# First group of a two-layer graph kernel: another order of loads, copies and sums; the last group's bias added in DRAM by one transfer

## The chip, the cores and the metric

The kernel runs on one core of one Trainium2 chip. The metric is the device time of one execution in microseconds (us); lower is better. The core has five engines that run side by side, each through its own list of instructions in order: PE (TensorE, matrix products; its loading of weights is listed apart as PEld), DVE (VectorE), ACT (ScalarE), POOL (GpSimd) and SP (SyncE, which here only issues transfers). ACT and POOL issue transfers too, between their other instructions. PE has a granted clock, which the profile gives as a share of full speed.

## The reference, cut to what matters

```python
# layer 0, four heads of 128; x is 4096 x 512, adj 4096 x 4096 of zeros and ones
support = (x @ weight) split in heads
f1, f2  = support . weight_u, support . weight_v          # one number per row and head
w       = leaky_relu(f1[column] + f2[row], 0.2) * adj
attn    = softmax(where(w != 0, w, -1e30)) * (w != 0)
x1      = layernorm(x + attn @ support + bias + x @ proj_w + proj_b)
# layer 1, eight heads of 64: masked attention on x1 with Wks, Wqs, Wvs, Wo
out     = layernorm(x1 + attention(x1, max(adj, eye)))
```

The change touches only the part before and at the start of layer 0's attention: `support`, the two dot products, and `base = x + x @ proj_w + bias + proj_b`, which is kept in DRAM and added when a window of rows is closed.

## The kernel before, in words

**Groups.** The 4096 rows are worked in eight groups `g` of 512 (loop L910). A group makes two products: kind "s" (`x @ weight`, into a tile `s4`) and kind "b" (`x @ (proj_w + I)`, into two tiles `base[0]` and `base[1]`; the identity, added to `proj_w` once by `add_identity`, stands for the `x +`). Each product is done by seven block products instead of eight (Strassen's scheme in Winograd's form), numbered 1 to 7. Products 1, 2, 4 (of x) and 1, 2, 3 (of the weights) use plain blocks, the others sums of blocks: four sums of x for each group (`combine_x`, numbers 0 and 1 on DVE, 2 and 3 on POOL) and four sums of the weights for each kind (`combine_w`), made once. `product` (L835) issues the eight matrix instructions of a block product as 2 x 2 calls at L846 and then its end: products 1 and 5 are copied from PSUM to SBUF by ACT (L863), product 2 by ACT to its place (L865), 6, 7, 3, 4 are added to what went before by DVE (L867, L869, L874), and POOL adds product 5 to one block (L871). Products 2, 3 and 4 add to the PSUM tiles of 1, 5 and 7, so product 2 cannot start before ACT has copied 1, nor 4 before DVE has read 7.

**Order.** The order of every engine is the order in which the program is written (`manual_schedule`). A list `plan` gives the order of the fourteen products of a group: `begin` for the first group, `usual` for the middle ones, `end` for the last. `beside`, `todo` and `early` hang other work on places in the plan: loads of the adjacency, the dot products (`dots`, eight pairs of instructions at L817 for each of four blocks, on DVE), the transposes of the next group's x (`turn_x`, DVE), and for the last group the first work of the attention (`signs` on ACT, `front` on DVE). `later` puts a piece of work a few steps on.

**First loads.** x and the weights come in quarters of 32 partitions. ACT's queue issues the first half of `weight` (four transfers), one quarter of x, the second half of `weight` (L664), then `weight_u`, `weight_v` and `bias`, each spread to all partitions (L676, L677). SP's queue issues the rest of the first group's x, `proj_w` (eight transfers) and the next group's x. [...] PE runs 46 idle transposes (L886) until the first data are there. The weights' sums of kind "s" are on DVE (L763), those of kind "b" on POOL after the identity (sixteen instructions at L895); POOL then adds `proj_b` to `bias` by an adding transfer (L905).

**Bias.** The sum `bb` of the two biases is added to `base[0]` and `base[1]` of each group at L879: by POOL, and in the last group by DVE. Each is then stored by SP (L881).

**Hand-over to the attention.** The attention of layer 0 goes over passes (window `w` of 1024 rows, head `h`) and 32 steps `j` in each. `front(w, h, j)` makes the tile of weights `p` of a step: two steps of signs on ACT (L624), a mask on DVE (L635), and one DVE instruction for each tile (L640); four tiles exist (`LA + 1`). `front` runs three steps ahead of PE's products (L1087): the first three tiles are made in the last group (`early`), the fourth in the first round of the loop at L1076. The adjacency goes through DRAM: POOL's transfer turns it to bf16 (`narrow`, L586), SP's transposes it into `stage` (`turn_in0`, L594), ACT shrinks it to fp8 (`shrink`, L600). Of the first window's eight pieces the last (piece 7) is issued by `beside_unit` in the first round of the loop; its transpose stands in SP's list behind that of piece 6, and `shrink` of pieces 6 and 7 stands in ACT's list among the signs.

Of the kernel before, what the change touches and what calls it, by code (L numbers as in the profile page):

```python
# [8 lines left out]
F32 = mybir.dt.float32  # L9
# [3 lines left out]
AF = mybir.ActivationFunctionType  # L13
ALU = mybir.AluOpType
# [4 lines left out]
P = 128  # L19
# [410 lines left out]
def tile_gat_then_masked_attention(  # L430
# [16 lines left out]
    nc = tc.nc  # L447
    N, D = x.shape
# [4 lines left out]
    NG = N // G  # L453
    GT = G // P
# [15 lines left out]
    NQ = P // SQ  # L470
# [33 lines left out]
    def on_all_partitions(src, n):  # L504
        return bass.AP(tensor=src.tensor, offset=src.offset, ap=[[0, P], [1, n]])
# [61 lines left out]
    with tc.tile_pool(name="l0", bufs=NG) as l0, \  # L567
# [3 lines left out]
        LA = 3  # L571
# [73 lines left out]
        with tc.tile_pool(name="l0s", bufs=2) as sp:  # L645
# [11 lines left out]
                        x[g * G + b0 * SQ:g * G + b1 * SQ, a * P:(a + 1) * P].rearrange(  # L657
                            "(b r) f -> r b f", r=SQ))

            def load_w0(queue, dst, src, c):  # L660

                for a in range(NQ):
                    f = a * P + 2 * c * SQ
                    queue.dma_start(  # L664
                        dst[a * SQ:(a + 1) * SQ, 2 * c:2 * c + 2, :],
                        src[f:f + 2 * SQ, :].rearrange("(k r) d -> r k d", r=SQ))
# [1 line left out]
            bb = sp.tile([P, D], F32, name="bb", bufs=1)  # L668
            load_w0(nc.scalar, w_sb, weight, 0)
            load_x(0, 0, HG // SQ, (nc.sync, nc.sync, nc.sync, nc.scalar))  # L670
            load_w0(nc.scalar, w_sb, weight, 1)
            load_x(0, HG // SQ, G // SQ)
            for c in range(2):
                load_w0(nc.sync, pw_sb, proj_w, c)
            for k, src in enumerate((weight_u, weight_v)):
                nc.scalar.dma_start(uv[:, k, :], on_all_partitions(src, D))  # L676
            nc.scalar.dma_start(bb, on_all_partitions(bias, D))  # L677
            load_x(1)

            def factors(g, s4):  # L680
# [41 lines left out]
            for c in range(NCJ):  # L722
# [4 lines left out]
                if c < NCJ - 3:  # L727
                    for k in range(CJ):
# [1 line left out]
                            lambda c=c, k=k: shrink(0, c, k))  # L730
            beside.setdefault(NT // 2, []).append(lambda: load_fr(0, 0))
            early = {5: lambda: signs(0, 0, 0), 8: lambda: front(0, 0, 0), 9: lambda: front(0, 0, 1),
                     7: lambda: signs(0, 0, 2), 11: lambda: front(0, 0, 2)}

            def turn_x(g, c, n=0, halves=1):

# [98 lines left out]
            def product(g, s4, kind, i):  # L835

                if i in (1, 5, 6, 7):
                    tiles[kind, i] = op.tile([P, G], F32, name="o_ps")  # L840
                out = tiles[kind, {2: 1, 3: 5, 4: 7}.get(i, i)]
                more = i in (2, 3, 4)
                xb, wb = x_of(g, i), w_of(kind, i)
                for t in range(2):
                    for c in range(2):
                        nc.tensor.matmul(out[:, t * HD:(t + 1) * HD], xb[:, c, t * P:(t + 1) * P],  # L846
                                         wb[:, c, :], start=not more and t == 0 and c == 0,
                                         stop=c == 1, skip_group_check=True)
                if i == 1:
                    if kind == "b":  # L850
                        for n in range(2):
                            base[n] = sp.tile([P, 2, D], F32, name="base", bufs=3)
                    elif g == NG - 1:
                        places = room("y_sb").rearrange("p s c r -> p s (c r)")
                        sb.update({("s", 1): places[:, 0], ("s", 5): places[:, 1],
                                   ("b", 1): places[:, 2], ("b", 5): places[:, 3]})
                    else:
                        sb.update({("s", 1): room("z"), ("s", 5): room("z"),
                                   ("b", 1): room("az"), ("b", 5): room("az")})
                u2, p5 = sb[kind, 1], sb[kind, 5]  # L860
                last = block_of(kind, s4, 1, 1)
                if i in (1, 5):
                    nc.scalar.activation(sb[kind, i], out, AF.Copy)  # L863
                elif i == 2:
                    nc.scalar.activation(block_of(kind, s4, 0, 0), as_block(out, kind), AF.Copy)  # L865
                elif i == 6:
                    nc.vector.tensor_tensor(u2, out, u2, op=ALU.add)  # L867
                elif i == 7:
                    nc.vector.tensor_tensor(last, as_block(out, kind), as_block(u2, kind),  # L869
                                            op=ALU.add)  # L870
                    nc.gpsimd.tensor_tensor(last, last, as_block(p5, kind), op=ALU.add)  # L871
                else:
                    n, m = (0, 1) if i == 3 else (1, 0)
                    nc.vector.tensor_tensor(block_of(kind, s4, n, m), as_block(out, kind),  # L874
                                            as_block(u2, kind), op=ALU.add)
                if kind == "b" and i in (3, 4):
                    n = (3, 4).index(i)
                    engine = nc.vector if g == NG - 1 else nc.gpsimd
                    engine.tensor_tensor(base[n], base[n],  # L879
                                            bb[:, None, :].to_broadcast([P, 2, D]), op=ALU.add)  # L880
                    later.at(1, lambda t=base[n]: nc.sync.dma_start(  # L881
                        base_d[g][:, 2 * n:2 * n + 2, :], t))

# [3 lines left out]
            for n in range(2):  # L887
                for c in range(KC):
                    turn_x(0, c, n, 2)
            def add_identity(m):  # L890
                for c in range(KC):
                    for a in range(2 * m, 2 * m + 2):
                        q, f = slice(a * SQ, (a + 1) * SQ), a * P + c * SQ
                        d = pw_sb[q, c, f:f + SQ]
                        nc.gpsimd.tensor_tensor(d, d, ident[q, q], op=ALU.add)  # L895

            combine_x(0, 0)
            combine_w(nc.vector, "s", (5,))
            for i in (1, 2, 3):
                combine_x(0, i)  # L900
            combine_w(nc.vector, "s", (6, 7, 4))
            for m in range(2):
                add_identity(m)
# [1 line left out]
            nc.gpsimd.dma_start(bb, on_all_partitions(proj_b, D), accum_op=ALU.add)  # L905
            uv_ps = [xp.tile([P, H0, D0], F32, name="x_ps") for _ in range(2)]
            usual = [(kind, i) for i in (1, 5, 2, 6, 7, 3, 4) for kind in ("s", "b")]
            begin = [(kind, i) for kind in ("s", "b") for i in (1, 2, 5, 6, 7, 3, 4)]
            end = [(kind, i) for kind in ("s", "b") for i in (1, 5, 2, 6, 7, 3, 4)]
            for g in range(NG):  # L910
                fs[g] = l0.tile([P, 2, GT, H0], F32, name="f")
                s4 = sp.tile([P, H0, GT, W0], F32, name="s4")
                plan = end if g == NG - 1 else usual if g else begin
                todo = {}
                for k, (i, wait, n, m) in enumerate(
                        ((2, 1, 0, 0), (3, 0, 0, 1), (7, 3, 1, 1), (4, 0, 1, 0))):
                    todo.setdefault(plan.index(("s", i)) + wait if g else 7 + k, []).append((n, m))
                for k, (kind, i) in enumerate(plan):
                    if k in (0, 3, 7, 10):
                        t = (0, 3, 7, 10).index(k)  # L920
                        if t == 1 and g + 2 < NG:
                            load_x(g + 2)
                        for fn in beside.get(g * GT + t, []):
                            fn()
                    product(g, s4, kind, i)
                    if g == 0 and k == 6:
                        for n in range(2):
                            nc.scalar.activation(uv_ps[n], uv[:, n, :].rearrange(
                                "p (h d) -> p h d", h=H0), AF.Copy)
                    for nm in todo.get(k, ()):  # L930
                        dots(g, s4, *nm)
                    if g == NG - 1 and k in early:
                        early[k]()
                    if g == NG - 1 and k == 10:
                        factors(g, s4)
                    first = 0 if g else 10
                    if g + 1 < NG and first <= k < first + KC:
                        turn_x(g + 1, k - first)
                    if g + 1 < NG and (6 <= k < 10 if g else k == 13):
                        for n in (k - 6,) if g else range(4):  # L940
                            combine_x(g + 1, n)
                    if k in (2, 6, 9, 12):
                        later.step()
                xTs.pop(g)
                x_s.pop(g)
                if g + 1 == NG:
                    later.step()
                if g + 1 < NG:
                    later.at(1, lambda g=g, s4=s4: factors(g, s4))

# [33 lines left out]
        with wait_by_tile("l0v", 2) as vp:  # L984
# [91 lines left out]
            for n, (w, h, j) in enumerate(steps):  # L1076
                if n + LA < len(steps):
                    beside_unit(*steps[n + LA])
                    front(*steps[n + LA])
                if j == 0:  # L1080
                    o_t[w, h] = [op.tile([P, G], F32, name="o_ps")[:, 0:BK * W0].rearrange(
                        "p (b d) -> p b d", b=BK) for _ in range((WT + BK - 1) // BK)]
# [709 lines left out]
```

## Time and profile before

| | us |
|---|---|
| three timed runs | 3325.18, 3324.55, 3321.34 |
| their median | 3324.55 |
| the profiled execution, its own time | 3324.41 |
| span of its instructions | 3322.5 |
| PE busy in the span | 3301.6 (99%) |
| DVE, POOL, ACT busy | 2477.7, 2173.3, 1947.7 |
| group 0: first product to the start of group 1 | 8.78 to 40.96 |
| groups 1 to 7 | 40.96 to 210.17 |
| layer 0's attention | from 210.17 |

The time is the span and 1.9 us around it. A row of the timeline has start, duration, engine, line, operation, what it writes and reads, and in brackets how long the engine was idle before it and what ended that. SPq, ACTq and POOLq are issues of transfers, whose durations are those of the issue and not of the transfer. A merged row stands for several instructions (x8). In a row of the view by windows each engine has its busy time in that stretch, then come the granted clock and the share of the DMA engines.

### The profile page before, as it was taken

The numbers are of one execution on the slowest core, as the hardware profiler recorded it, in microseconds if no ns is written. First come the engines' busy times: TensorE is split into PE (matmuls) and PEld (weight loads), VectorE is DVE, ScalarE is ACT, GpSimd is POOL, SyncE is SP. The second block draws the span as 40 slices with busy tenths as digits, with TensorE's granted clock in tenths as the row PEclk, the third lists the DMA queues.
The fourth block names the chain that finished last, engine by engine and source line by source line (L and its number), as shares of the span: only waits on it lengthen the run. The fifth ranks groups of instructions, "written<-read, shape, count | busy, mean of one in ns | idle before, by whom it ended". The sixth has DMA issues, their size and how long they took to land.

```text
span 3322.5 us, 67217 instructions
## 1 busy us (share of the span) xinstructions
PE 3301.6 (99%) x27160; PEld 1967.0 (59%) x27160; DVE 2477.7 (75%) x3186; ACT 1947.7 (59%) x2439; POOL 2173.3 (65%) x1602
## 2 busy tenths in 40 slices
PE   9999999999999999999999999999999999999998
PEld 8899999999999777733333333333333333333333
DVE  6689899899999677467767666677666766667766
ACT  1267968878766310156656566566665656656564
POOL 5630040040030244389999999999999999999996
PEclk9999999999999999999999999999999999999999
DMA  8989796686532444489898988889889799897984
GB/s 178 227 204 183 220 182 170 153 191 147 138 93 58 104 146 125 153 221 208 193 211 224 228 195 198 209 188 259 198 197 211 187 215 242 196 210 185 214 195 112
DMA packets 398993, 612.06 MB, mean 184 GB/s; under 512 B 167632, under 2 KB 248528, under 8 KB 398672
## 3 DMA queue, kind: packets, MB, share of 16 engines
q0 software_dynamic: 97520, 258.77, 42.8%
q1 hardware_dynamic: 299280, 345.88, 33.5%
q8 instruction: 216, 3.54, 0.4%
q10 hardware_dynamic: 1872, 3.02, 0.4%
q14 instruction: 105, 0.86, 0.1%
HBM read 315.87 MB, written 109.25 MB: 128 GB/s over the span
## 4 chain that ended last, share of the span: by engine, by line
PE 97%; DVE 1%; DMA 1%; POOL 1%; issue 0%; ACT 0%; ACTq 0%; POOLq 0%; DVEq 0%
PE o_ps L1087 27%; PE o_ps L1599 26%; PE s_ps L1138 26%; PE o_ps L846 5%; PE s_ps L1663 3%; PE s_ps L1298 2%; PE s_ps L1248 2%; PE s_ps L1255 2%; PE x_ps L1255 1%; PE x_ps L1248 1%; PE s_ps L1618 1%; DMA p<-p 0%; PE s_ps L1294 0%; DMA w_sb<-in_L_gnn_weight_dram 0%; DVE p L1731 0%
## 5 line engine op out<-in xcount | busy, mean ns | idle before, releaser
L1574 POOL TENSOR_TENSOR q_sum<-q_sum,p 128x1024 f32<-128x1024 f32 x538 | 1375.6, 2557 | 64.3 <-DMA p<-p 39.5
L1554 DVE TENSOR_TENSOR p<-s_ps,adjT 128x1024 f32<-128x1024 f32 x896 | 1044.5, 1216 | 465.0 <-ACT s_ps L1551 436.2
L1551 ACT ACTIVATE s_ps<-s_ps 128x1024 f32<-128x1024 f32 x1021 | 967.2, 1006 | 594.4 <-PE s_ps L1138 591.9
L1599 PE MATMUL o_ps<-p,v_sb 64*64 64x512 f32 x8192 | 943.6, 590 | 0.0
L1138 PE MATMUL s_ps<-q_sb,k_sb 64*64 64x512 f32 x8192 | 942.9, 589 | 0.1
L1087 PE MATMUL o_ps<-sup_t,p 128*128 128x129 f32 x8192 | 915.7, 275 | 1.2 <-DVE p L640 1.2
L1087 PEld LDWEIGHTS o_ps<-sup_t,p 128*128 128x128 f32 x8192 | 915.3, 192 | 1.7 <-DVE p L640 1.4
L640 DVE SCALAR_TENSOR_TENSOR p<-fr_t,dj,az 128x1024 f32<-128x1024 f32 x512 | 650.3, 1284 | 66.9 <-PE o_ps L1087 38.8
L1599 PEld LDWEIGHTS o_ps<-p,v_sb 64*64 64x64 f32 x8192 | 310.3, 133 | 570.6 <-issue 560.6
L1138 PEld LDWEIGHTS s_ps<-q_sb,k_sb 64*64 64x64 f32 x8192 | 312.6, 133 | 566.4 <-issue 453.9
L624 ACT ACTIVATE z<-fr_t,f 128x1024 fp8e4<-128x1024 f32 x512 | 557.1, 1143 | 100.9 <-DVE az L635 100.8
L1584 POOL DMA_DIRECT2D p<-p x412 | 438.6, 1303 | 10.1 <-PE o_ps L1599 9.2
L1063 POOL DMA_DIRECT2D agg<-base_d x32 | 29.1, 1217 | 386.8 <-DMA sup_t<-sup_d 204.7
L585 POOL COPY seen<-token 128x1 f32<-128x1 f32 x24 | 10.9, 455 | 356.8 <-DVE token L583 356.8
L1554 DVE TENSOR_TENSOR p<-s_ps,md 128x1024 f32<-128x1024 f32 x128 | 150.7, 1217 | 67.8 <-ACT s_ps L1551 62.0
L635 DVE TENSOR_TENSOR az<-adjT,z 128x512 int32<-128x512 int32 x256 | 175.2, 685 | 2.1 <-ACT z L624 0.9
L600 ACT ACTIVATE adjT<-stage 128x1024 fp8e4<-128x1024 bf16 x128 | 130.9, 1051 | 18.3 <-DMA stage<-adj_d 18.2
L1663 PE MATMUL s_ps<-wo_sb,on 128*128 128x512 f32 x240 | 110.8, 604 | 0.0
L1633 ACT ACTIVATE r<-r_h 32x256 f32<-32x256 f32 x248 | 102.2, 412 | 2.9
L1049 ACT ACTIVATE agg<-o_ps,rinv 128x128 f32<-128x128 f32 x128 | 42.1, 370 | 70.5 <-DVE den L1042 46.3
L1322 ACT ACTIVATE v<-s_ps 128x256 f32<-128x256 f32 x28 | 10.7, 383 | 115.0 <-PE s_ps L1298 99.9
L1663 PEld LDWEIGHTS s_ps<-wo_sb,on 128*128 128x128 f32 x240 | 43.3, 189 | 55.9 <-issue 55.7
(275 smaller groups left out, 2236.0 us busy)
## 6 DMA issues: line engine op xcount, KB each, us to landing
p<-p POOLq DMA_DIRECT2D x412, 512.0 KB, 9.1
k_sb<-k_d SPq DMA_DIRECT2D x128, 512.0 KB
v_sb<-v_d SPq DMA_DIRECT2D x128, 512.0 KB
adj_d<-in_adj_dram POOLq DMA_DIRECT2D x32, 1024.0 KB, 11.0
sup_t<-sup_d SPq DMA_DIRECT2D x120, 258.0 KB
fr_t<-fr_d SPq DMA_DIRECT2D x16, 1024.0 KB
adjT_d<-adjT SPq DMA_DIRECT2D x32, 512.0 KB
adjT<-adjT_d SPq DMA_DIRECT2D x32, 512.0 KB
```

What stands on the lines that cost most here:

```text
L624: nc.scalar.activation(z[:, k, :], fr_t[w, h][:, 0, :], AF.Sign, bias=fs[j // GT][:, 0, (j + k) % GT, h:h + 1], saturate=False)
L635: nc.vector.tensor_tensor(az.bitcast(I32), adjT[w, j // CJ][:, j % CJ:j % CJ + 2, :].bitcast(I32), z.bitcast(I32), op=ALU.bitwise_and)
L640: nc.vector.scalar_tensor_tensor(p, fr[:, 1, :], dj[j // GT][:, j % GT, h:h + 1], az_t[w, h, j // 2][:, j % 2, :], op0=ALU.max, op1=ALU.mult)
L846: nc.tensor.matmul(out[:, t * HD:(t + 1) * HD], xb[:, c, t * P:(t + 1) * P], wb[:, c, :], start=not more and t == 0 and c == 0, stop=c == ...
L1087: nc.tensor.matmul(o[t // BK][:, t % BK, :], p[:, t * P:(t + 1) * P], s, start=(j == 0 and t % BK == 0), stop=(j == NT - 1), skip_group_ch ...
L1138: nc.tensor.matmul(s[c:c + MS, e, :], k[r, a + c:a + c + MS], qt[g, m][r, :], start=True, stop=True)
L1551: nc.scalar.activation(s, s, AF.Exp, scale=float(KD) ** -0.5)
L1554: nc.vector.tensor_tensor(p, s, keep[:, None, :].to_broadcast([P, HP, G]), op=ALU.mult)
L1574: nc.gpsimd.tensor_tensor(q, q, p, op=ALU.add)
L1584: later.at(2, lambda: nc.gpsimd.dma_start(a, b, accum_op=ALU.add))
L1599: nc.tensor.matmul(o[c, n, :], v[r, j % CH, c], p[r, e, :], start=(j == 0), stop=(j == NT - 1))
L1663: nc.tensor.matmul(s, on_t[g][:, m, t * P:(t + 1) * P], wo_sb[:, m, :], start=(m == 0), stop=(m == NP1 - 1))
```

## The change

- **Loads.** SP issues the first two quarters of the second half of `weight` ahead of the second half of the first x; ACT issues only the other two. `weight_u`, `weight_v` and `bias` are issued by POOL, between and after its two sums of x.
- **ACT's table.** A copy of one column (`ones`, into a small tile) is put on ACT ahead of its last two loads, so that the load of ACT's function table stands there.
- **DVE's first sum of weights** (number 5 of kind "s") stands between the transposes of the two halves of x.
- **Plan of the first group.** Kind "b" goes 1, 5, 2, 6, 7, 3, 4 instead of 1, 2, 5, 6, 7, 3, 4.
- **Last group's bias.** The two DVE additions are gone. After the group's last step POOL issues one adding transfer that adds `bb`, repeated four times, to `base_d[7]` in DRAM; it waits for the stores of both base tiles. Piece 7 of the adjacency stands behind it in POOL's list.
- **Fourth tile of weights.** `front(0, 0, 3)` is put in the last group, after product 3 of kind "b" and ahead of DVE's end of product 4; the loop's first round leaves it out.

```diff
-            def load_w0(queue, dst, src, c):
+            def load_w0(queue, dst, src, c, quarters=range(NQ)):
-                for a in range(NQ):
+                for a in quarters:
...
             load_w0(nc.scalar, w_sb, weight, 0)
             load_x(0, 0, HG // SQ, (nc.sync, nc.sync, nc.sync, nc.scalar))
-            load_w0(nc.scalar, w_sb, weight, 1)
+            load_w0(nc.sync, w_sb, weight, 1, range(2))
+            nc.scalar.activation(small.tile([P, 1], F32, name="bn_ve"), ones[:, 0:1], AF.Copy)
+            load_w0(nc.scalar, w_sb, weight, 1, range(2, NQ))
             load_x(0, HG // SQ, G // SQ)
             for c in range(2):
                 load_w0(nc.sync, pw_sb, proj_w, c)
-            for k, src in enumerate((weight_u, weight_v)):
-                nc.scalar.dma_start(uv[:, k, :], on_all_partitions(src, D))
-            nc.scalar.dma_start(bb, on_all_partitions(bias, D))
             load_x(1)
...
             early = {5: lambda: signs(0, 0, 0), 8: lambda: front(0, 0, 0), 9: lambda: front(0, 0, 1),
-                     7: lambda: signs(0, 0, 2), 11: lambda: front(0, 0, 2)}
+                     7: lambda: signs(0, 0, 2), 11: lambda: front(0, 0, 2), 12: lambda: front(0, 0, 3)}
...
                 if kind == "b" and i in (3, 4):
                     n = (3, 4).index(i)
-                    engine = nc.vector if g == NG - 1 else nc.gpsimd
-                    engine.tensor_tensor(base[n], base[n],
-                                            bb[:, None, :].to_broadcast([P, 2, D]), op=ALU.add)
+                    if g < NG - 1:
+                        nc.gpsimd.tensor_tensor(base[n], base[n],
+                                                bb[:, None, :].to_broadcast([P, 2, D]),
+                                                op=ALU.add)
...
             for n in range(2):
                 for c in range(KC):
                     turn_x(0, c, n, 2)
+                if n == 0:
+                    combine_w(nc.vector, "s", (5,))
...
             combine_x(0, 0)
-            combine_w(nc.vector, "s", (5,))
-            for i in (1, 2, 3):
+            for i in (1, 2):
                 combine_x(0, i)
+            for k, src in enumerate((weight_u, weight_v)):
+                nc.gpsimd.dma_start(uv[:, k, :], on_all_partitions(src, D))
+            combine_x(0, 3)
+            nc.gpsimd.dma_start(bb, on_all_partitions(bias, D))
             combine_w(nc.vector, "s", (6, 7, 4))
...
-            begin = [(kind, i) for kind in ("s", "b") for i in (1, 2, 5, 6, 7, 3, 4)]
             end = [(kind, i) for kind in ("s", "b") for i in (1, 5, 2, 6, 7, 3, 4)]
+            begin = [("s", i) for i in (1, 2, 5, 6, 7, 3, 4)] + end[7:]
...
                 if g + 1 == NG:
                     later.step()
+                    nc.gpsimd.dma_start(base_d[g], bb[:, None, :].to_broadcast([P, GT, D]),
+                                        accum_op=ALU.add)
...
                     beside_unit(*steps[n + LA])
-                    front(*steps[n + LA])
+                    if n:
+                        front(*steps[n + LA])
```

## The prediction

> **What bounds the kernel now.** First the page: busy times, then the chain that ended last.
>
> ```profile
> PE 3301.6 (99%) x27160; PEld 1967.0 (59%) x27160; DVE 2477.7 (75%) x3186; ACT 1947.7 (59%) x2439; POOL 2173.3 (65%) x1602
> ...
> PE 97%; DVE 1%; DMA 1%; POOL 1%; issue 0%; ACT 0%; ACTq 0%; POOLq 0%; DVEq 0%
> ```
>
> PE is the bound: it is idle 3322.5 - 3301.6 = 20.9 us in all. The first real product starts at 8.78 and the last 12 us are the closing of the kernel, neither of which the change touches. What is left is small, so I read where PE waits in the two places that the diff touches, with the timeline. The first group:
>
> ```profile
> 8.78 1.99 PE L846 MATMUL o_ps<-w_sb,xT 128*128 128x256 f32 x8
> ...
> 11.82 0.33 ACTq L677 DMA_DIRECT2D bb<-in_L_gnn_bias_dram  x1
> 12.19 1.28 ACT L863 ACT_TABLE_LOAD   x1 [12.19 <-DMA w_sb<-in_L_gnn_weight_dram]
> ...
> 13.48 0.60 ACT L863 ACTIVATE z<-o_ps 128x512 f32<-128x512 f32 x1
> 14.13 3.78 PE L846 MATMUL o_ps<-w_sb,xT 128*128 128x256 f32 x8 [3.36 <-ACT z L863]
> ```
>
> Product s1 ends at 10.77. s2 adds to the same PSUM tile and waits 3.36 us for ACT's copy, and ACT is late because its last three issues (9.52, 10.63, 11.82) each wait for a quarter of the second half of the weights, with the table load behind them. s2 then takes 3.6 us where eight instructions take 1.72 later on. The view by windows says why:
>
> ```profile
> 10.80:12.80 2.00, 0.00 (x0) 0.00 (x0) 1.20 (x4) 0.61 (x1) 0.34 (x1) 1.00 1.07 246
> 12.80:14.10 1.30, 0.00 (x0) 0.00 (x0) 1.27 (x2) 1.27 (x2) 0.92 (x1) 0.51 1.06 277
> 14.10:16.30 2.20, 2.17 (x5) 1.81 (x6) 2.20 (x5) 0.00 (x0) 0.75 (x1) 0.50 1.04 302
> 16.30:19.60 3.30, 3.30 (x9) 2.58 (x9) 2.10 (x2) 0.60 (x1) 2.94 (x7) 0.50 1.12 218
> 19.60:23.00 3.40, 3.40 (x18) 2.99 (x17) 0.60 (x1) 1.61 (x3) 2.71 (x12) 0.99 1.20 185
> ```
>
> After 2.0 us of idleness the granted clock falls to half, until 19.6; PE works from 14.13 to 19.65 at half speed and loses 5.5 / 2 = 2.7 us. What ends the group:
>
> ```profile
> 28.76 1.39 POOL L871 TENSOR_TENSOR s<-s,z 128x512 f32<-128x512 f32 x1
> ...
> 35.46 0.69 DVE L867 TENSOR_TENSOR az<-o_ps,az 128x512 f32<-128x512 f32 x1 [1.80 <-PE o_ps L846]
> 37.73 0.71 DVE L740 STREAM_TRANSPOSE xT<-y_sb 128x512 f32<-128x512 f32 x1
> 38.36 0.65 DVE L869 TENSOR_TENSOR base<-o_ps,az 128x512 f32<-128x512 f32 x1
> ...
> 39.16 1.97 PE L846 MATMUL o_ps<-more_w,xT 128*128 128x256 f32 x8 [0.35 <-DVE base L869]
> ```
>
> b4, the last product, waits for DVE. From 40.96 PE runs without a gap to the attention, whose fourth step waits:
>
> ```profile
> 214.42 1.23 DVE L879 TENSOR_TENSOR base<-base,bb 128x1024 f32<-128x1024 f32 x1 [0.56 <-POOL base L871]
> ...
> 215.56 1.28 DVE L640 SCALAR_TENSOR_TENSOR p<-fr_t,dj,az 128x1024 f32<-128x1024 f32 x1
> ...
> 216.90 9.29 PE L1087 MATMUL o_ps<-sup_t,p 128*128 128x129 f32 x79 [1.20 <-DVE p L640]
> ```
>
> **The change, part by part.** Sums are made against the profiled execution, 3324.41 us, 0.14 under the median.
>
> *Front of group 0.* ACT's table load moves to about 4.3, behind the issue at 3.93, and ends at 5.6; its next issue waits for a transfer that lands at 5.7, so it is hidden, and 1.28 is its price without that cover. uv and bias leave ACT, so the copy of s1 runs at 10.8 to 11.45. The weights' second half is issued at 2.16, 4.29, 5.74 and 7.48 in place of 5.44 to 8.28; by the landings in the trace a piece issued at 7.48 to 7.59 was there at 11.4 to 11.8. So s2 starts near 11.7 instead of 14.13, a gap of 0.9. The price: the last piece of x's second half goes from 7.48 to about 7.85, landing near 12.0 instead of 11.4, and DVE's second transposes start at 12.2 instead of 11.60. The sum 5 that moves between them (0.68) falls into DVE's 1.89 us of idleness and is free. s5 needs DVE's sum of x: 12.2 + 1.46 + 1.13 = 14.8. PE, done with s2 at 13.4, waits about 1.5 us and then has full work: eleven products of 1.72 to the end of b3, 33.8.
>
> *POOL is next.* It gets three issues. The row of the same form is L905: 1.07 long, the next instruction 0.81 after it (27.95 to 28.76); L1584's issues take 1.30 each. I take 0.81, the pitch of the same form, and 1.30 as the other end. First sum of x 13.05 to 14.3; two issues to 15.95; second sum 1.61 to 17.55 (its 1.83 us of idleness before goes into the issues); bias 18.35; identity 5.77 (17.16 to 22.93) to 24.1; four sums 5.02 (22.93 to 27.95) to 29.15; proj_b 0.81; s-sum L871 1.2, done at 31.2 instead of 30.15. Kind b in the order 1, 5, 2 removes PE's 0.73 at 29.94, but asks POOL's first sum (24.1 + 1.27 = 25.4) one product earlier; b1 ends at 25.2, so 0.3 is given back. uv is needed by ACT at 23.5; issued by 16, a form that takes 4.58 to land has it at 21.
>
> *DVE behind POOL.* The dots of the block that L871 completes stand ahead of everything DVE does for b6 and b7, so POOL's 31.2 sets the end: eight dots 1.67, az 0.61, eight dots 1.66, transpose 0.63, base 0.65, 0.15 to PE: b4 starts at 36.7, not 39.16. PE could have started at 34.2. **Group 0 gives 2.5 us**, less than the 3.36 + 2.7 + 0.73 that disappear on PE, since a wait of 2.5 us for POOL and DVE takes their place. Ends: with issues of 1.30 POOL is 1.5 later and the gain 1.0; if POOL never binds, b4 starts at 34.2 and the gain is 5.0. The new wait may halve the clock once more. Lost then: half of a stretch of 3.4 (as much as one row's 6.8 / 2), 1.7; nothing if not.
>
> [...]
>
> *Last group.* Two DVE additions go (1.35 + 1.23, and 0.56 of waiting for POOL); the fourth p (1.28) moves ahead of DVE's end of b4. It is ready near 213.8, in old times, against PE's 215.7: **1.2 us** go. Late next is the fifth p: about 216.4 against 217.5, no stall. b4's base store comes about 1.3 later behind p, but the 2.6 of additions ahead of it go.
>
> *The adding transfer.* POOL waits for both base stores, and piece 7 of the adjacency stands behind. Before, that piece was issued at 214.33 and landed at 226.94. Now, on a clock 2.5 earlier: stores issued at 212.9 and 213.4, landing near 216.9 (2.64 each alone, 42.79 to 45.43). An addition in DRAM is not in the trace; the nearest are L1584's, 512 KB between SBUF tiles: 4.5 to 16.8, median 9.1. For 1 MB I take 9.1, since little else is in flight then, with 4.5 and 18 (twice the median) as ends. Landed at 226; piece 7, right behind it in the queue, 5.5 later at 231.5 (its quickest row is 8.2 from issue to landing, and I let the queue hide a third); its transpose 7.0 to 9.2 (the row at 228.5, and the one at 295.6 beside another adjacency load): 238.5 to 240.7. ACT comes to shrink it at 242.13 - 3.7 = 238.4. PE needs the signs behind it only 3.3 us later (step 24 at 254.5, 2.0 for DVE, signs ready at 249.2 before). Limit 241.7: **no cost**, with 1 to 3 us of margin.
>
> [...]
>
> Sum: 3324.41 - 2.5 - 1.2 = **3320.7**.
>
> **The rivals.**
> *A, the forecast (0.50):* 3320.7, own range 3319 to 3322.5.
> *B, POOL does not bind (0.18).* For it: its waits of 1.83 now take in the issues. 3324.41 - 5.0 - 1.2 = 3318.2; with a piece of x landing earlier, 3317.5.
> *C, the gain is eaten (0.20).* POOL's issues take 1.30 and the clock halves in the wait ahead of b4: 3324.41 - 1.0 - 1.2 + 1.7 = 3323.9. For it: 2.0 us of idleness were enough at 12.8. That the change does not do what it says belongs here too: if s2 is held by a quarter of weights and not by ACT, the time is that of before.
> *D, slower (0.12).* The adding transfer takes 16.8 instead of 9.1: piece 7's transpose lands at 247 to 248, past 241.7, ACT stands before its shrink with the signs behind it, and PE waits 6.7 in the attention. 3324.41 - 3.7 + 6.7 = 3327.4, with the clock 3329. It decides from 10 to 12 us for that transfer. Against it: the stores finish before it is issued, and only piece 6's transpose is beside it.
>
> **How the numbers follow.** A is likeliest: 3320.7. The range takes in A, B and C and leaves D out: 3317.8 to 3325.5. A measurement of this kernel can tell about 0.2% (6.6 us) from no change. Faster by that is under 3317.9: half of B, 0.10. Slower is over 3331.2: the worst of D, 0.05. Within: 0.85.
>
> **What would show it.** ACT's table load near 4.3; PE's wait before the second product under 1.2 with the clock at 1.00 to 20 us; b4 at 36 to 37.5 after a wait of 2 to 3 us put down to DVE, and POOL's L870 ending near 31; no wait before the attention's fourth step; ACT's wait for stage under 3 us. Wrong if PE waits at L1087 between 225 and 260, or if b4 starts before 35 or after 38.5.

## The result and the profile after

| | before | after |
| --- | --- | --- |
| median of the runs shown | 3324.98 us (17 runs, 3321.34 to 3328.19) | 3330.55 us (17 runs, 3329.55 to 3333.70) |
| once more, beside each other | 3324.84 us (27 runs) | 3331.13 us (11 runs) |
| profiled execution | 3324.41, span 3322.5, clock 0.998 | 3331.82, span 3330.0, clock 0.997 |

The ratio is 1.0017 with a 95% interval of 1.0011 to 1.0024, and 1.0016 (1.0007 to 1.0025) in the second measurement. (A ratio takes in all runs, so it need not be that of the medians.) The changed kernel is 5.6 to 6.3 us slower. The forecast was 3320.7, with a range of 3317.8 to 3325.5.

PE's waits in after, over the whole span (first number: us in all; then how often; then the longest):

```profile
PE o_ps L1095 <- DVE p L640: 5.8, 1, 5.8
PE o_ps L845 <- DVE p L796: 2.1, 1, 2.1
PE s_ps L1146 <- DVE p L1562: 1.8, 3, 1.0
PE o_ps L845 <- DVE base L868: 1.5, 1, 1.5
...
PE o_ps L845 <- ACT z L862: 0.7, 1, 0.7
```

L845 is the product of the groups (L846 in before), L1095 the product of the attention (L1087 in before), L1146 the scores of layer 1. The new first line is the result: one wait of 5.8 us in the attention. Of before's waits the 3.4 for ACT's copy is down to 0.7, and the 1.2 ahead of the attention's fourth step is gone.

PE in the first group of after, from its timeline (start, length, engine and line, and in brackets the wait before it):

```profile
8.94 2.00 PE L845 MATMUL o_ps<-w_sb,xT 128*128 128x256 f32 x8 [0.70 <-DVE xT L739]
11.62 1.99 PE L845 MATMUL o_ps<-w_sb,xT 128*128 128x256 f32 x8 [0.69 <-ACT z L862]
15.67 3.72 PE L845 MATMUL o_ps<-fr_t,p 128*128 128x256 f32 x16 [2.06 <-DVE p L796]
...
36.44 1.97 PE L845 MATMUL o_ps<-more_w,xT 128*128 128x256 f32 x8 [1.51 <-DVE base L868]
```

The second product starts at 11.62 (before: 14.13), b4 at 36.44 (39.16), and the attention at 207.46 (210.17). The granted clock was 1.00 throughout. Here the change does what was forecast. The loss is in the timelines of POOL, ACT and PE, here in the order of cause and effect. POOL first, before and then after:

```profile
214.33 0.79 POOL L586 DMA_DIRECT2D adj_d<-in_adj_dram  x1
...
236.29 0.76 POOL L586 DMA_DIRECT2D adj_d<-in_adj_dram  x1
```

```profile
218.35 1.30 POOL L953 DMA_DIRECT2D base_d<-bb  x1 [6.67 <-DMA base_d<-base]
219.05 1.38 POOL L586 DMA_DIRECT2D adj_d<-in_adj_dram  x1
230.83 0.57 POOL L585 COPY seen<-token 128x1 f32<-128x1 f32 x1 [10.40 <-DVE token L583]
231.34 0.76 POOL L586 DMA_DIRECT2D adj_d<-in_adj_dram  x1
```

The adding transfer (L953) holds POOL until the base stores have landed, and piece 7 of the adjacency (L586 at 219.05; before at 214.33) stands behind it. By the landings in the trace the adding transfer took 8.45 us, piece 7 was there at 232.79 and its transpose could be issued at 232.84. One and a half microseconds before that, at 231.34, POOL had issued the first piece of window 1. The transpose took 14.58 and landed at 247.43 (before: 6.96, at 235.47). Then ACT, which shrinks the piece (before, and after with its wait for the transpose), and PE, two engines further on:

```profile
242.13 1.04 ACT L600 ACTIVATE adjT<-stage 128x1024 fp8e4<-128x1024 bf16 x1
```

```profile
247.45 1.06 ACT L600 ACTIVATE adjT<-stage 128x1024 fp8e4<-128x1024 bf16 x1 [12.95 <-DMA stage<-adj_d]
```

```profile
243.75 3.18 PE L1095 MATMUL o_ps<-sup_t,p 128*128 128x129 f32 x27
252.75 9.50 PE L1095 MATMUL o_ps<-sup_t,p 128*128 128x129 f32 x63 [5.82 <-DVE p L640]
```

ACT's signs for the next steps stand behind the shrink, DVE's weights `p` behind the signs, PE behind the weights. The clock was halved from 250.53 to 257.36, and PE worked 4.6 us of that at half speed, as this table of stretches shows (length, PE's busy time and matmuls, granted clock, DMA share, GB/s):

```profile
242.00:246.90 4.90, 4.90 (x45) 1.00 1.31 166
246.90:250.50 3.60, 0.03 (x1) 1.00 1.12 333
250.50:252.70 2.20, 0.00 (x0) 0.51 1.10 274
252.70:257.40 4.70, 4.65 (x22) 0.50 1.07 375
257.40:262.00 4.60, 4.60 (x44) 1.00 0.47 88
```

In 4.7 us it did 22 matmuls, and 44 in the 4.6 behind that. The balance of two pairs of profiled executions, each stretch from the start of one matmul to the start of another:

| stretch | before | after | | before, again | after, again | |
| --- | --- | --- | --- | --- | --- | --- |
| first product to attention | 201.39 | 198.52 | -2.9 | 199.95 | 199.06 | -0.9 |
| attention of all windows, first to last matmul | 916.65 | 923.00 | +6.3 | 916.64 | 923.34 | +6.7 |
| layer 1, first scores to last matmul of the kernel | 1907.81 | 1911.21 | +3.4 | 1909.92 | 1909.51 | -0.4 |
| last matmul to the end of the span | 12.56 | 12.96 | +0.4 | 11.93 | 12.85 | +0.9 |

What is left (the start of the first product, 275.3 us between attention and scores) differs by less than 0.3. So there are three things to explain: a gain in the first group that is not the same in each execution, a loss of 6.5 in the attention that is, and something in layer 1 that one pair shows and the other doesn't.

### The profile page after: what moved, and what is told of

Its sections match the earlier page's. It is cut to its first block, busy times and chain, and to the rows that moved or that the text cites. A ratio compares the mean times of both kernels' runs of the same rounds, so it can differ in the third digit from the quotient of the medians.

```text
span 3330.0 us, 67212 instructions
## 1 busy us (share of the span) xinstructions
PE 3301.1 (99%) x27160; PEld 1966.8 (59%) x27160; DVE 2476.6 (74%) x3184; ACT 1948.2 (59%) x2440; POOL 2175.0 (65%) x1606
## 4 chain that ended last, share of the span: by engine, by line
PE 85%; POOL 3%; DMA 3%; issue 1%; DVE 1%; ACT 1%; POOLq 0%; DVEq 0%
PE o_ps L1095 26%; PE o_ps L1607 23%; PE s_ps L1146 23%; PE s_ps L1671 3%; DMA p<-p 2%; PE s_ps L1306 2%; POOL q_sum L1582 2%; PE s_ps L1256 2%; PE s_ps L1263 2%; PE x_ps L1263 1%; POOL p L1592 1%; PE x_ps L1256 1%; PE s_ps L1626 0%; ACT z L624 0%; DMA stage<-adj_d 0%
## 5 line engine op out<-in xcount | busy, mean ns | idle before, releaser
L1146 PE MATMUL s_ps<-q_sb,k_sb 64*64 64x512 f32 x8192 | 944.1, 589 | 1.9 <-DVE p L1562 1.8
L1095 PE MATMUL o_ps<-sup_t,p 128*128 128x129 f32 x8192 | 917.5, 276 | 5.8 <-DVE p L640 5.8
L1095 PEld LDWEIGHTS o_ps<-sup_t,p 128*128 128x128 f32 x8192 | 917.3, 192 | 6.1 <-DVE p L640 6.0
L1146 PEld LDWEIGHTS s_ps<-q_sb,k_sb 64*64 64x64 f32 x8192 | 312.4, 133 | 569.4 <-issue 452.8
```

Of the source, the lines that this page charges most:

```text
L1095: nc.tensor.matmul(o[t // BK][:, t % BK, :], p[:, t * P:(t + 1) * P], s, start=(j == 0 and t % BK == 0), stop=(j == NT - 1), skip_group_ch ...
L1146: nc.tensor.matmul(s[c:c + MS, e, :], k[r, a + c:a + c + MS], qt[g, m][r, :], start=True, stop=True)
```

## The experiments

The theory (T1) after the comparison: the adding transfer's wait delays piece 7 on POOL, the delayed transpose meets window 1's first load, and PE's wait and the halved clock follow; the first group and the early fourth weights are gains. Rivals: the 1 MB of the adding transfer slows the transposes (V), the first group's edits cost something later (S), layer 1 has the loss (L).

**The last group's edits alone** (kernel before, with the L953 transfer, without DVE's additions, with `front(0, 0, 3)` early):

> The kernel before with the edits of the last group and the attention alone: no additions of the bias on DVE, the adding transfer, layer one's fourth weights ahead of it. T1: all of the loss and none of the first group's gain: -1.2 for the wait before the fourth step, +5.8 for the wait, +2.3 for the halved clock, +6.9 in all, about 3332. Rival S (the first group's edits, with loads of x that land later, shift the DMA queues and cause the loss): -1.2, about 3324.

Measured 3333.01 beside 3326.0 (33 runs of before): ratio 1.0020, 1.0011 to 1.0029, that is +7.0. The wait is 5.7, the attention takes 923.76, and the transpose 13.90 beside a load issued 2.06 ahead of it. S falls: all of the loss is here.

**The first group's edits alone:**

> The kernel before with the edits of the first group alone; the last group and the attention as before. T1: group 1 starts 2.7 us earlier and nothing is lost later, about 3322.3 (-2.7). Rival S: the loss is here, 3327 or more. Rival G (the gain of 2.7 is eaten later, by a wait that the earlier start only moves): within 1 us of before.

Measured 3324.01: -2.0, ratio 0.9995 (0.9986 to 1.0004), which doesn't tell -2.7 from nothing. In the profile the stretch from the first product to the attention takes 198.09 and the attention 916.38, no more than before's 916.65. Against S.

**First group's edits and the early fourth weights, with DVE's additions kept:**

> The kernel after with the bias added in the last group by DVE's two additions, as before, and no adding transfer; the fourth weights are still ahead. T1: the first group's 2.7 and the 1.2 of the attention's fourth step together, about 3321.1 (-3.9). Rival E (the early fourth weights are worth nothing, since the additions on DVE stand ahead of them): as with the first group's edits alone, -2.7. Rival S: 3327 or more.

Measured 3325.94: -0.1, ratio 0.9997 (0.9988 to 1.0006). The early weights are not worth 1.2 here, they lose about 2: the attention takes 918.58. DVE's and PE's timelines say why:

```profile
210.32 2.29 DVE L640 SCALAR_TENSOR_TENSOR p<-fr_t,dj,az 128x1024 f32<-128x1024 f32 x1
212.54 0.68 DVE L873 TENSOR_TENSOR base<-o_ps,y_sb 128x512 f32<-128x512 f32 x1
213.32 1.23 DVE L878 TENSOR_TENSOR base<-base,bb 128x1024 f32<-128x1024 f32 x1
...
215.25 2.48 DVE L640 SCALAR_TENSOR_TENSOR p<-fr_t,dj,az 128x1024 f32<-128x1024 f32 x2
```

```profile
216.59 5.59 PE L1092 MATMUL o_ps<-sup_t,p 128*128 128x129 f32 x33 [1.87 <-DVE p L640]
```

The fourth `p` is ready earlier, and the additions that stood ahead of it now stand ahead of the fifth: the wait moves one step on and grows from 1.2 to 1.87, and the clock fell behind it from 216.8 to 220.2 (0.61 in the stretch from 216 to 219.5). Here a new order on DVE only moved the wait; in the kernels without the additions (after, and those below) it is gone.

**Piece 7's load ahead of the adding transfer:**

```diff
                 if g + 1 == NG:
                     later.step()
+                    narrow(0, NCJ - 1)
                     nc.gpsimd.dma_start(base_d[g], bb[:, None, :].to_broadcast([P, GT, D]),
                                         accum_op=ALU.add)
...
-                    if j == LA:
-                        narrow(0, NCJ - 1)
```

> The kernel after with one thing moved: the seventh (last) adjacency load of window 0 is issued on POOL ahead of the adding transfer, so that it doesn't stand behind the transfer's wait for the base stores. Theory T1 (that wait, 6.67 us in the trace of after, holds the load on POOL, its transpose lands at 247.43 instead of 235.47, and the matmuls of the attention wait 5.8 us and then run 6.8 us at half clock): the wait of L1095 is gone, time about 3320.5 to 3322, that is -3 to -4.5 against before. Rival V (the 1 MB that the adding transfer moves slows the transposes whatever the order): a wait of 3 us or more stays, time at or above 3325. Rival L (the loss comes behind the attention's start, in layer 1's waits of 1.8 + 1.1 us, from changed orders elsewhere): wait gone in the attention, time still 3325 or more.

Measured 3328.1: +2.1, ratio 1.0006 (0.9997 to 1.0015), where after itself is 5.6 to 6.3 over before. The one wait became three smaller ones, and no clock fell in the attention (918.65):

```profile
236.99 11.38 PE L1094 MATMUL o_ps<-sup_t,p 128*128 128x129 f32 x96 [0.83 <-DVE p L640]
250.09 3.84 PE L1094 MATMUL o_ps<-sup_t,p 128*128 128x129 f32 x32 [1.72 <-DVE p L640]
254.15 8.05 PE L1094 MATMUL o_ps<-sup_t,p 128*128 128x129 f32 x70 [0.22 <-DVE p L640]
```

T1 in this form failed. Piece 7 landed at 224.19, but now the adding transfer itself (223.63 to 234.10) ran ahead of the transpose, which took 18.91 and landed at 244.76. It isn't the queue on POOL alone; it is what POOL moves while the transpose runs, and V is partly right.

**Window 1's first load behind the transpose.** After, with this load 6 steps later and everything else, the adding transfer too, in its place:

```diff
-  if u == (13 + 5 * (c - 3) if w else 16 + 5 * c) and c >= min(3, 3 * w):
+  if u == (13 + 5 * (c - 3) if w else 16 + 5 * c + 6 * (c == 0)) and c >= min(3, 3 * w):
```

> The kernel after with one thing moved: window 1's first adjacency load, which ran beside piece 7's transpose (231.34 to 240.43 against 232.84 to 247.43), is issued 6 steps of the attention later, behind window 1's second load. Theory T1 in its full form (the adding transfer delays the transpose, and a casting load beside it doubles its time from 7 to 14.6): piece 7's transpose takes 7 to 10 and lands near 241, the wait of L1095 falls from 5.8 to 1.5 or less, the clock isn't halved, time 3323 to 3326, at least 5 under after. Rival V (the transpose is slow beside the other loads on SP or behind the adding transfer alone): a wait of 4 or more stays, time within 2 of after.

Measured 3323.01 beside 3325.05: ratio 0.9999 (0.9990 to 1.0008), 7.5 under the first median of after. One of the eleven runs took 3333.81, the others at most 3326.11. The adding transfer took 8.44, piece 7 landed at 232.84, both as in after. The transpose took 6.23 and landed at 239.12, and from there ACT and PE:

```profile
239.14 1.06 ACT L600 ACTIVATE adjT<-stage 128x1024 fp8e4<-128x1024 bf16 x1 [4.56 <-DMA stage<-adj_d]
```

```profile
207.54 54.66 PE L1095 MATMUL o_ps<-sup_t,p 128*128 128x129 f32 x488
```

PE runs 54.66 us without a gap. The attention takes 914.71, which is 8.3 less than in after: the wait of 5.82 and some 2.5 for the halved clock and what goes with it. So rival L falls too: the loss goes with the wait, while layer 1 (1910.16) is no shorter than before's (1907.81 and 1909.92). Measured again beside after:

> The same kernel as the one with window 1's first load later, measured once more beside after itself. T1: again a transpose under 8, no wait of L1095, 5 to 8 under after and 1 to 4 under before.

3323.59 against 3331.13 of after and 3324.84 of before (0.9999, 0.9990 to 1.0008); transpose 6.17, attention 914.71 (again one run apart, at 3334.78). This is the version that beats after, by 7.5. Against before its 1.3 to 2.0 are within the interval.

> The kernel after, once more, beside the other two and for a second profiled execution. T1: the transpose of piece 7 beside window 1's first load again 13 to 16, the wait of L1095 again 5 to 6.5, the clock halved behind it; 4 to 7 above before. If the halved clock is chance: the wait without it, and 2 less.

Measured 3331.13, ratio 1.0016 (1.0007 to 1.0025): the transpose took 14.59, the wait was 5.8, and the clock was halved behind it from 251.78 to 258.6, as in the kernel with the last group's edits alone (from 251.48, for 6.83). All three profiles of these two kernels have the wait and the halved clock.

**The load beside the transpose in the kernel before.** No edit of the change, but window 1's first load 4 steps earlier, and then 6 (in the same line, `- 4 * (c == 0)` and `- 6 * (c == 0)`):

> The kernel before, without any edit of the change, but with window 1's first adjacency load issued 4 steps of the attention earlier (about 229.7 instead of 236.3), so that it runs beside piece 7's transpose (228.5 to 235.5 in before). Theory T1 (a casting load beside a transpose is what doubles it): the transpose takes 12 to 15 instead of 6.96 and lands at 240 to 243.5; ACT's wait for stage grows from 2.5 to 8 or more; since that is at the limit of 241.7 that the prediction worked out, PE waits 0 to 2 there, time 0 to 4 above before. Rival V (the transpose needs the adding transfer near it to be slow): 7 to 9, no wait, time as before.

Measured 3326.71 beside 3324.84: 1.0003 (0.9994 to 1.0012). The transpose took 9.10, not 12 to 15: issued at 227.92, with the load 1.83 behind it. ACT waited 2.2 for `stage`, not 8 or more, and PE for nothing new in the attention.

> The kernel before, without any edit of the change, with window 1's first adjacency load issued 6 steps earlier (about 226.5), 1 to 2 ahead of piece 7's transpose as in after, and not 1.8 behind it as in the kernel with 4 steps, where the transpose took 9.10. Theory T2 (it is the load that stands ahead of the transpose that doubles it; behind it, the load waits instead): the transpose takes 13 to 16 and lands at 241 to 244.5, ACT waits 8 to 11 for stage, PE waits 0 to 3 there, time 0 to 5 above before. Rival V (a load beside it costs 2 whatever the order, the rest of after's 14.6 comes from the adding transfer): 8 to 10, no wait for p beyond the fourth step's 1.2, time within 1 of before.

Measured 3325.95 beside 3325.54: 1.0001 (0.9992 to 1.0010). The load was issued at 224.54, the transpose 1.62 behind it at 226.17; it took 12.19, a little under the range, and the load 10.56. It landed at 238.36, as it had started earlier than in after; ACT waited 3.7, not 8 to 11, and PE only the 1.2 of before's fourth step. Why it takes 12.19 here and 14.58 in after was not tested. All of piece 7's transposes, by the landings:

| kernel | transpose | us | POOL's transfer beside it |
| --- | --- | --- | --- |
| after with the load 6 steps later, twice | 232.89, 232.90 | 6.23, 6.17 | none |
| before, twice | 228.52, 227.60 | 6.96, 6.94 | none until it had landed |
| before, load 4 steps earlier | 227.92 | 9.10 | load, issued 1.83 behind |
| before, load 6 steps earlier | 226.17 | 12.19 | load, issued 1.62 ahead |
| last group's edits alone | 233.18 | 13.90 | load, issued 2.06 ahead |
| after, twice | 232.84, 233.29 | 14.58, 14.59 | load, issued 1.50 and 1.45 ahead |
| after, piece 7's load first | 225.85 | 18.91 | adding transfer, 2.22 ahead, and load 5.15 behind |

Against before's 6.96, a load of 1 MB issued 1.5 to 2.1 ahead of this transpose went with 5 to 8 us more, one that followed by 1.8 with 2, and the adding transfer with a load behind it with 12. The transpose of piece 6, one earlier, shows the same in all 18 profiles. Piece 7's load was issued 2.0 to 2.7 ahead of it in twelve, among them both of before: 15.2 to 17.1. In one it was 3.5 ahead: 13.24. In the five that have the adding transfer at the group's end it came 5.3 to 5.6 behind: 7.96 to 9.43.

**The adding transfer in the attention,** at step 70 of window 0's 128, from a row in DRAM that a 2 KB store fills:

```diff
-                    nc.gpsimd.dma_start(base_d[g], bb[:, None, :].to_broadcast([P, GT, D]),
-                                        accum_op=ALU.add)
+                    nc.sync.dma_start(bb_d, bb[0:1, :])
...
+                if w == 0 and u == 70:
+                    nc.gpsimd.dma_start(base_d[NG - 1], row, accum_op=ALU.add)
```

> The kernel after with the adding transfer moved into the attention of window 0 (step 70 of its 128), where nothing waits for POOL; the sum of the biases goes to a row in DRAM by a 2 KB store at the end of the last group, and the late transfer reads that row. Everything else as in after. T1: piece 7's load and transpose go as before the change, no wait of L1095 between 225 and 260 and none before the fourth step; what is left is the first groups' gain, the 1.2 and layer 1's 1.8 of new waits: 2 to 4 under before. Rival V2 (1 MB read and written beside window 1's loads costs as much there): a new wait of 3 or more in steps 70 to 90, time above before.

Measured 3324.34 beside 3325.05: 0.9997 (0.9988 to 1.0006). The transfer took 20.3 us at 294.5. A transpose issued beside it, at 305.23, took 14.60, where the one at that place takes 7.64 in after, and ACT waited 6.5 for it, but PE had no wait there. The attention takes 915.49, piece 7's transpose 6.83. V2 falls. Of the 2 to 4 that were to be left the median shows 0.7, with an interval that takes in both 0 and 4.

**The first group's halved clock.**

> The kernel before once more, for a second profiled execution. In the one shown the clock was halved from 12.83 to 19.66 and the attention started 203.2 us behind the first product; in the kernel with the last group's edits alone, whose first group is the same, the clock wasn't halved there and the attention started 200.4 behind it, as in the kernels with the first group's edits (200.1 to 200.3). If the halving is what mostly happens in before: again near 203.2, and the first group's gain is the halving that goes. If it was chance: near 200.4, and the first group's edits are worth 0.2.

(This text counts from PE's first wait for data, some 2 us ahead of the first matmul; from matmul to matmul its 203.2 is 201.39, its 200.4 is 198.27, and its 200.1 to 200.3 are 197.98 to 198.52.) Between the two: 199.95, with the clock halved for 3.41 us from 13.86. Five profiles of kernels with before's first group took 201.39, 199.95, 198.27, 200.64 and 198.51 from the first product to the attention (halved for 6.83, 3.41, 0, 3.41 and 0 us; mean 199.8). Eight with the changed one took 197.84 to 199.06 (mean 198.3), halved once, for 3.41, in the longest. So the edits are worth 1.5 on average: 2.9 against one execution and nothing against another. Where the clock wasn't halved, 198.27 and 198.51 stand against 197.84 to 198.52.

**Layer 1.** From first scores to last matmul it took 1907.8 to 1909.9 in the five profiles (mean 1908.75) and 1908.8 to 1911.6 in the eight (mean 1910.06): 1.3 more, with ranges that overlap. One stretch on DVE shows it: 569.9 to 570.7 in the five, 570.6 to 573.1 in the eight. The texts below call its ends the 200th and the 800th masked product; they are the 200th and the 800th entry of that line, waits counted, and 311 of the 896 masked products lie between. In after PE waited there for DVE's `p` (1.0 us, not at all in before); DVE waited there, ACT apart, for the transfers of POOL's sums (5.5, in before 1.4) and for POOL's additions (2.7, in before 6.6). One move of the first group at a time:

> The kernel before with one edit of the first group alone: the loads of weight_u, weight_v and bias on POOL's queue at their new place, instead of ACT's. All four kernels with the first group's edits show waits of 0.9 to 2.5 us for DVE p in the second pair of heads of layer 1 (near 1665 to 1730), which before and the kernel with the last group's edits alone don't show. Theory M (three more DMAs on POOL's queue shift its accumulating transfers of layer 1 against SP's loads): the same waits, layer 1 1 to 2 longer than in before. Rival N (it comes from another edit of the first group, or it is chance): no wait near 1665 to 1730. In the first group: POOL is the later by about 2.4 of issues, b4 1 to 2.5 later, time 1 to 4 over before.

Measured 3324.32 beside 3325.05 (0.9996, 0.9987 to 1.0005), not slower as expected. The stretch took 569.88, so by this measure M falls. But what lies behind it was 1 to 2 longer than in the five (1124.65 to the last entry of that line, against 1122.69 to 1123.75), and layer 1 as a whole, 1910.33, is as long as in the eight: M isn't settled.

> The kernel with the first group's edits alone, but with the loads of weight_u, weight_v and bias back on ACT's queue, where before has them. Measured by the stretch of layer 1 between the 200th and the 800th masked product on DVE: 569.9, 570.7, 569.9, 569.9 and 570.4 in five profiles without the first group's edits, 570.6 to 573.1 in eight with them. Theory M (the three DMAs more on POOL's queue lengthen layer 1): 569.9 to 570.4. Rival W (it is the quarters of weight on SP's queue, or another order): 570.8 or more.

> The same kernel with the three loads back on ACT, a second profiled execution: within 0.5 of the first look if the kernel sets the stretch, not if it is chance.

> The kernel with the first group's edits alone, but with the first two quarters of weight's second half on ACT's queue instead of SP's. Same measure. Theory W (two DMAs more on SP's queue): 569.9 to 570.4. Theory M or another: 570.8 or more.

> The same kernel with the two quarters back on ACT, a second profiled execution: within 0.5 of the first look if the kernel sets the stretch, not if it is chance.

With the three loads back on ACT the stretch took 570.65 and 571.04, with the two quarters back on ACT 571.89 and 571.36 (single times 3327.45, 3326.16, 3324.14, 3323.21). Neither undoes it clearly; 570.65 and 571.04 lie at the edge. What makes layer 1 some 1.3 us longer stays open; both of these kernels keep the other edits of the group. One thing they did show: with the three loads back on ACT, PE waited 4.2 and 3.8 for DVE's `p` in the first group, and from the first product to the attention it took 202.34 and 200.80; with the two quarters back on ACT it took 198.99 and 197.03. So the first group's gain needs the three loads off ACT's queue, and the quarters' move to SP's shows no gain.

## Why the prediction was wrong

- **First group: the path right, the baseline not.** ACT's table load at 4.2, the second product at 11.62 (11.7 forecast), POOL's L870 done at 31.05 (31.2), b4 at 36.44 (36.7): -2.7 in the profile for -2.5 forecast. The issue times in its sum are rows of before, and there they follow landings: the first eight transfers of ACT and SP were issued from 0.73 to 2.17, the next eight each 0.02 behind a landing (3.93 behind 3.91, and so on to 7.84 behind 7.82). Its two new waits were 2.06 ahead of the third product (1.5 forecast) and 1.51 ahead of b4 (2 to 3). But the 2.5 was the halved clock of the one execution that was shown. The mean of five profiles against eight is 1.5, and against an execution of before's first group without the halving it is about nothing.
- **Fourth `p`: right, for the reason that wasn't weighed.** The wait is gone, and with window 1's load out of the way the attention gains 1.9 (916.65 to 914.71), not 1.2: 1.6 of it by the fifth step. With the adding transfer at step 70 it gains 1.2. The early weights alone, with the additions kept, lose 2, since the additions then stand ahead of the fifth `p`: it is their removal that makes the term right.
- **The adding transfer itself: right.** Stores landed at 217.76 (216.9), the transfer took 8.45 (9.1; 8.45 to 8.89 in the five profiles that have it at that place), piece 7 was there at 232.79 (231.5).
- **The step that failed: "its transpose 7.0 to 9.2".** It took 14.58, and PE's wait at 252.75 is the prediction's own sign of being wrong. The prediction took the 9.2 from "the row [...] at 295.6 beside another adjacency load". By the landings that load was issued at 298.17, 2.59 behind the transpose: the cheap order, which measured 9.10 again in the experiment. And it didn't see that the load comes ahead at all. Window 1's first load is issued when DVE's token of step 16 comes, behind its 16th `p`. The attention started 2.7 earlier and DVE, rid of the additions, gained another 2.5 by that `p` (234.69, now 229.47); so that load was issued 5.0 earlier (236.29, now 231.34), while piece 7 came 4.3 later (transpose issued at 228.52, now 232.84). Two edits moved towards each other. Before's trace had the costly order too, in the transpose just ahead of the row that was read: piece 6's, issued at 216.37 with piece 7's load 2.04 ahead of it, took 15.69. And it had transposes of 10.72 and 13.13 (issued at 102.39 and 127.20) whose loads came 8.2 and 7.5 behind, so the order isn't all that counts; what lengthened those was not tested. Any of the three would have widened the range.
- **The limit of 241.7: right.** 247.43 less the wait of 5.82 is 241.6, and the landings at 238.36 and 239.12 cost nothing. ACT came to the shrink at 234.5 and not at 238.4, so its wait, which was to stay under 3, was 12.95 in after, and 4.56 where the load was moved and nothing was lost.
- **Rival D: right result, wrong mechanism.** It had the transpose landing at 247 to 248, a wait of 6.7, and 3329 with the clock; but it priced the adding transfer at 16.8 for that, and "decides from 10 to 12 us for that transfer" kept its chance at 0.12. At 8.45 it happened all the same, so the numbers it came near are luck.
- **Layer 1: not in the sum at all.** Some 1.3 us by the profiles, with ranges that overlap; cause open.
- **The clock behind short waits: open in the forecast, open still.** It fell behind a wait of 1.87 (the early fourth weights, additions kept: 0.61 from 216 to 219.5), and behind a wait of 2.07 in one execution of after but not behind 2.06 in the other (1.00 from 13.6 to 24). The 1.7 for one more halving was an estimate, half of a stretch of 3.4; halved stretches of 3.41 us were measured (first group of before, again, and of after, again) and of 6.83 (first group of before, attention of after).

## What to carry to other kernels

When an edit frees an engine, follow every transfer that this engine's progress releases: it starts earlier, and may now stand ahead of one that another edit has made later. A price "beside" other traffic needs the order with it: look up which of the two was issued first (here 12.19 to 14.59 us with the load ahead of the transpose, 9.10 with it 1.83 behind). And before a sum takes a stall of one profiled execution as its gain, ask whether the stall is there in every execution: the halved clock was there in three of five executions of before's first group.

## What the runs showed that was not expected

A 1 MB transfer that casts or adds on POOL's queue, issued 1.5 to 2.2 us ahead of a DMA transpose, went with transposes of 12.2 to 18.9 us, where the same piece took 6.2 or 7.0 with none beside it; issued 1.8 behind, with 9.1. The adding transfer took 8.45 us at the group's end, 10.47 beside two transposes, and 20.3, from a row in DRAM, amid window 1's loads.
